# Attention under one named ScalarE table set, with the tanh of a row's gated input in three stretches a head later

## The chip, the core and the metric

One NeuronCore of a Trainium2 chip runs the whole network as one program. The time is the device time of one execution, in microseconds (us). Engines named below: PE (TensorE: matmuls, with PEld its weight loads), ACT (ScalarE: functions by table, copies, scalings), DVE (VectorE), POOL (GpSimd), SP (SyncE, which issues most DMAs). Each engine works through its own list of instructions in order; instructions on different engines wait for each other through semaphores.

## The reference, cut to what matters

Four rows (batch elements) of 512 tokens and 512 channels go through a Mamba-style layer, a mixture of experts, an attention layer and a feed-forward layer. Each layer takes its input through a gate, a bidirectional decayed sum over the tokens. Only the last two layers and the gate matter here:

```python
# the gate (r: the residual stream; k = v: a side input)
ek  = exp(minimum(k, 30)); ekv = ek * v
nf, df, nb, db = ...        # scans of ekv and ek over the tokens, both ways
euk = exp(minimum(u + k, 30))
num = nf + nb - ekv + euk * v
den = df + db - ek + euk
gate = sigmoid(r) * (num / maximum(den, 1e-8)) * (0.8 + 0.2 * tf)

# attention on h = gate(x): 16 heads in 4 groups, head size 128, causal
q = h @ w_q; k, v = split(h @ w_kv)
probs = softmax(where(causal, q @ k.T * scale, -inf))
x = x + (probs @ v) @ w_dense

# feed-forward on h = gate(x)
x = x + (silu((h @ gate_w.T) * gate_s) * ((h @ up_w.T) * up_s)) @ down_w.T * down_s
...
```

## The kernel before, in words

Everything is float32. Activations lie with the channels on the 128 partitions, in four chunks of 128, and the 512 tokens of a row along the free axis. A planner places the instructions of each engine: the program's order gives priorities, and an instruction goes to its engine's list when its inputs are expected; `after(engine)` and `issue_after` pin an instruction behind another.

**Table sets.** [...] The class `Tables` (lines 96 to 128) names sets explicitly: `act.use(set)` writes a load of the set behind every function called through `act(...)` since the last load, and every later `act(...)` is written behind that load. `LOG_EXP` has exp and ln, `EXP` has exp and tanh, `SILU` has silu and tanh. After `act.leave()` no set is named, and the compiler puts in whatever loads the list needs. In the kernel before, all of the mixture of experts, the attention and the feed-forward layer runs in that state. A call through `act(...)` is recorded at line 121 while no set is named and at line 125 while one is; a named load is recorded at line 112.

**Gates.** The generator `gate_pair` makes the x-independent factor of a gate for two of the four chunks of one row: two side inputs, four forward scans (L256) and four backward scans (L262) on DVE, the scaled copies `f` (L258) and the exponentials `eu` on ACT, then the division as three passes of ACT over 1024 elements (`rec`): a Relu (L313), a Ln and an Exp (both recorded at L121), and three products on DVE (L319, L323, L328). The result is stored to DRAM (L330). `nudge()` takes one step of this work; the attention calls it once for each 128-query block of each head. `have(gate)` takes steps until a named gate is complete. `gated(l, b, ...)` calls `have`, loads the finished factor (L395) and applies it: a tanh on ACT for each chunk (L121, from `xr` into `th`) and a product on DVE (L383).

**Attention** (lines 1498 to 1658). The 64 heads run in the order group, row, head of the group. In each turn of the loop:

- for the second head of a row in the first group, `combine(b + 1)` adds the expert results to the next row: a scaling on ACT (L1442), a sum on DVE (L1443), four PE transposes (`pcb`, L1448) and an addition to the residual (L1452), for each of four token blocks; right after it `gated(2, b + 1, ...)` makes the next row's input `h`;
- `begin(n + 1)` makes the next head's queries (`pq`, L1552; `qT`, L1560), and at a new row its keys and values (`pk`, L1530; `pv`, L1538);
- `scores`: for each of four query blocks one matmul (`psc`, L1569), the causal mask (L1572), the negated row maximum (`nmax`, L1574), then Exp on ACT with the row sum (L1579), a reciprocal (L1580) and a scaling (L1581);
- `context` of the head before: ten PE transposes (`ptp`, L1592), four copies (`pT`, L1595, on ACT or DVE as the planner likes), four matmuls (`pctx`, L1601) and a copy (`cx`, L1609);
- after the fourth head of a row, `dense` of that row: 16 matmuls (`pd`, L1616) and four additions (L1624).

`pk`, `pv`, `pq` and `psc` share four PSUM buffers (`mm`), taken in turn: a matmul into one of them waits until the Exp or copy that reads its previous content is done.

**Feed-forward** (lines 1661 to 1711). The weights `ffg`, `ffu`, `ffd` are loaded into the room that the attention leaves. For each row `gated(3, b, ...)`, then 11 pairs of matmuls (`pfg` L1678, `pfu` L1683), a Silu (L1687), a product (L1688) and the down projection (`pfo`, L1693).

## Time and profile before

| what | value |
|---|---|
| median of three runs (lowest to highest) | 2603.02 us (2601.29 to 2605.94) |
| the profiled execution's own time | 2605.88 us |
| its span, first to last instruction | 2604.2 us |
| attention, about 1173 to 2147 us of the span | PE busy 941.1 of 974 us, DVE 535.5, ACT 437.9 |
| feed-forward, 2147 to 2604 us | PE busy 452.7 of 457 us |
| loads of a table set in the attention | 20 around Ln (10 at L121, 10 at L1579), 1 before the first Silu, 1.28 us each |

All times below count from the start of the span. The span is 1.7 us shorter than the execution's own time, and the execution is 2.9 us above the median. A line of the timeline gives the start, the length, the engine, the line of the kernel, the operation, and in brackets the engine's idle time just before it and the instruction it waited for.

### The profile page before, as it was taken

The numbers are of one execution on the slowest core, as the hardware profiler recorded it, in microseconds if no ns is written. First come the engines' busy times: TensorE is split into PE (matmuls) and PEld (weight loads), VectorE is DVE, ScalarE is ACT, GpSimd is POOL, SyncE is SP. The second block draws the span as 40 slices with busy tenths as digits, with TensorE's granted clock in tenths as the row PEclk, the third lists the DMA queues.
The fourth block names the chain that finished last, engine by engine and source line by source line (L and its number), as shares of the span: only waits on it lengthen the run. The fifth ranks groups of instructions, "written<-read, shape, count | busy, mean of one in ns | idle before, by whom it ended". The sixth has DMA issues, their size and how long they took to land.

```text
span 2604.2 us, 24554 instructions
## 1 busy us (share of the span) xinstructions
PE 2450.3 (94%) x8204; PEld 1300.7 (50%) x8204; DVE 1412.3 (54%) x2788; ACT 1033.2 (40%) x2126; POOL 259.9 (10%) x299
## 2 busy tenths in 40 slices
PE   3889998999989999989999999999999999999999
PEld 1555555556544444435555555555555554444444
DVE  8798898996345565556666654556553441011010
ACT  4576757666123233224454444345443431000000
POOL 1031223322211121210000000000000000000000
PEclk9989999999899999999999999999999999999999
DMA  6222423324244697876221101111000012000000
GB/s 216 82 93 94 166 74 126 130 69 146 82 177 170 217 371 296 334 242 219 61 65 45 45 29 29 45 41 33 21 25 16 17 53 97 17 0 16 8 8 16
DMA packets 91391, 259.82 MB, mean 100 GB/s; under 512 B 9857, under 2 KB 19457, under 8 KB 80641
## 3 DMA queue, kind: packets, MB, share of 16 engines
q1 hardware_dynamic: 82080, 231.51, 25.5%
q0 software_dynamic: 6880, 22.55, 2.4%
q10 hardware_dynamic: 2304, 4.20, 0.4%
q8 instruction: 65, 1.06, 0.2%
q14 instruction: 62, 0.50, 0.1%
HBM read 284.82 MB, written 47.05 MB: 127 GB/s over the span
## 4 chain that ended last, share of the span: by engine, by line
PE 77%; DVE 14%; ACT 4%; DMA 3%; issue 2%; POOL 0%; SPq 0%; ACTq 0%; DVEq 0%; POOLq 0%
PE pd L1616 8%; PE pq L1552 7%; PE pfu L1683 6%; PE pfo L1693 6%; PE pfg L1678 6%; PE pctx L1601 5%; PE pn L774 5%; PE pg L763 5%; PE po L796 4%; PE pc L995 4%; PE psc L1569 3%; PE po L1223 3%; PE pv L1538 2%; PE ptp L1592 2%; PE pk L1530 2%; PE pz L1066 2%
## 5 line engine op out<-in xcount | busy, mean ns | idle before, releaser
L1552 PE MATMUL pq<-h,wq 128*128 128x512 f32 x512 | 249.4, 603 | 9.5 <-ACT pr L1579 9.4
L1616 PE MATMUL pd<-cx,wd 128*128 128x512 f32 x512 | 222.4, 592 | 0.0
L995 PE MATMUL pc<-h,wxb 128*128 128x512 f32 x320 | 150.0, 624 | 45.8 <-DVE h L1263 38.7
L1687 ACT ACTIVATE hd<-pfg,cols 128x512 f32<-128x512 f32 x44 | 30.3, 688 | 381.0 <-PE pfg L1678 381.0
L1688 DVE SCALAR_TENSOR_TENSOR hd<-pfu,cols,hd 128x512 f32<-128x512 f32 x44 | 33.0, 751 | 269.2 <-PE pfu L1683 269.1
L1572 DVE TENSOR_TENSOR psc<-psc,mask 128x128 f32<-128x128 f32 x256 | 71.7, 287 | 196.1 <-PE psc L1569 196.0
L1579 ACT ACTIVATE pr<-psc,nmax 128x128 f32<-128x128 f32 (+3 forms) x256 | 135.3, 529 | 98.1 <-DVE nmax L1574 97.3
L1601 PE MATMUL pctx<-pT,v 128*128 128x512 f32 (+3 forms) x512 | 155.9, 448 | 7.5 <-ACT pT L1595 4.0
L1683 PE MATMUL pfu<-h,ffu 128*128 128x512 f32 x352 | 158.7, 592 | 0.9 <-DMA ffu<-in_upT 0.9
L1678 PE MATMUL pfg<-h,ffg 128*128 128x512 f32 x352 | 158.6, 592 | 0.0
L796 PE MATMUL po<-w,yT 128*128 128x512 f32 x312 | 145.3, 607 | 12.7 <-ACT yT L789 12.7
L1569 PE MATMUL psc<-kT,qT 128*128 128x128 f32 (+3 forms) x512 | 151.8, 436 | 2.2 <-ACT qT L1560 1.2
L1616 PEld LDWEIGHTS pd<-cx,wd 128*128 128x128 f32 x512 | 96.1, 190 | 114.8 <-issue 110.5
L1693 PE MATMUL pfo<-hd,ffd 128*128 128x512 f32 x352 | 151.7, 592 | 0.0
L763 PE MATMUL pg<-w,hT 128*128 128x512 f32 x312 | 145.1, 605 | 6.7 <-DMA w<-in_w1x 6.7
L1601 PEld LDWEIGHTS pctx<-pT,v 128*128 128x128 f32 x512 | 94.6, 193 | 99.2 <-issue 37.4
L774 PE MATMUL pn<-w,hT 128*128 128x512 f32 x312 | 141.0, 593 | 1.7 <-DMA w<-in_w1x 1.7
L1624 DVE TENSOR_TENSOR xr<-xr,pd 128x512 f32<-128x512 f32 x64 | 44.0, 688 | 175.5 <-PE pd L1616 175.5
L1574 DVE TENSOR_REDUCE nmax<-psc 128x1 f32<-128x128 f32 (+3 forms) x256 | 123.4, 484 | 2.7
L1552 PEld LDWEIGHTS pq<-h,wq 128*128 128x128 f32 x512 | 87.8, 193 | 68.4 <-issue 57.4
L1592 PEld LDWEIGHTS ptp<-ident,pr 128*128 128x128 f32 x640 | 78.3, 143 | 86.9 <-issue 40.4
L995 PEld LDWEIGHTS pc<-h,wxb 128*128 128x128 f32 x320 | 61.8, 199 | 118.2 <-issue 73.0
(305 smaller groups left out, 4217.4 us busy)
## 6 DMA issues: line engine op xcount, KB each, us to landing
w<-in_w1x SPq DMA_DIRECT2D x80, 1024.0 KB
w<-in_w2x SPq DMA_DIRECT2D x40, 1024.0 KB
wb<-in_b1x SPq DMA_DIRECT2D x40, 512.0 KB
lm<-cs SPq DMA_DIRECT2D x32, 512.0 KB
kt<-in_fT SPq DMA_DIRECT2D x62, 256.0 KB
ek<-ek SPq DMA_DIRECT2D x62, 256.0 KB
ekv<-ekv SPq DMA_DIRECT2D x62, 256.0 KB
g<-num SPq DMA_DIRECT2D x30, 512.0 KB
```

Of the source, the lines that this page charges most:

```text
L763: nc.tensor.matmul(pg, lhsT=hT[:, k, :], rhs=self.w1[s][0][:, k, :], start=(k == 0), stop=(k == NC - 1))
L774: nc.tensor.matmul(pn, lhsT=hT[:, k, :], rhs=self.w1[s][1][:, k, :], start=(k == 0), stop=(k == NC - 1))
L796: nc.tensor.matmul(po, lhsT=yT[:, j, :], rhs=self.w2[s][:, j, :], start=(j == 0), stop=(j == NI - 1))
L995: nc.tensor.matmul(pc, lhsT=wxb[:, k, m * P : (m + 1) * P], rhs=h[:, k, :], start=(k == 0), stop=(k == NC - 1),)
L1552: nc.tensor.matmul(pq, lhsT=u.wq[:, k, i * KVC : (i + 1) * KVC], rhs=u.h[:, k, :], start=(k == 0), stop=(k == NC - 1),)
L1569: nc.tensor.matmul(psc[:, :n], lhsT=qT[:, qi * P : n], rhs=u.kT[:, :n], start=True, stop=True)
L1579: nc.scalar.activation(pr, psc[:, :n], AF.Exp, bias=nmax, accum_out=rsum)
L1601: nc.tensor.matmul(pctx[:, kj * P :], lhsT=u.v[:, kj, :], rhs=pT[:, kj, kj * P :], start=(kj == 0), stop=(kj == NT - 1),)
L1616: nc.tensor.matmul(po, lhsT=u.wd[:, i, m * P : (m + 1) * P], rhs=u.ctxT[i], start=(i == 0), stop=(i == HPG - 1),)
L1678: nc.tensor.matmul(pg, lhsT=wg[:, k, cs], rhs=h[:, k, :], start=(k == 0), stop=(k == NC - 1))
L1683: nc.tensor.matmul(pu, lhsT=wu[:, k, cs], rhs=h[:, k, :], start=(k == 0), stop=(k == NC - 1))
L1693: nc.tensor.matmul(po, lhsT=wdn[:, i, m * P : (m + 1) * P], rhs=hd[i], start=(i == 0), stop=(i == NFF - 1),)
```

## The change

The attention names its table sets. `LOG_EXP` is loaded ahead of the first head, and the Exp of the scores (L1579) and the Silu of the feed-forward layer (L1687) go through `act(...)`, so that they stand behind the named loads, too. `gated(2, b + 1, ...)` moves from the turn of a row's second head to that of its third, behind `begin(n + 1)`, between a load of `EXP` and a load of `LOG_EXP`; `combine(b + 1)` stays where it was. After the last head `SILU` is loaded.

```diff
-                nc.scalar.activation(pr, psc[:, :n], AF.Exp, bias=nmax, accum_out=rsum)
+                act(pr, psc[:, :n], AF.Exp, bias=nmax, accum_out=rsum)
...
+        with after(nc.scalar):
+            act.use(act.LOG_EXP)
         groups = {}
         ready, held = begin(0), None
         for n, (g, b, i) in enumerate(heads_):
             u, qT = ready
             if g == 0 and i == 1 and b + 1 < B:
                 combine(b + 1)
-                hs[b + 1] = gated(2, b + 1, x[b + 1], gp, tag="h", name=f"h2_{b + 1}")
             if n + 1 < len(heads_):
                 ready = begin(n + 1)
+            if g == 0 and i == 2 and b + 1 < B:
+                act.use(act.EXP)
+                hs[b + 1] = gated(2, b + 1, x[b + 1], gp, tag="h", name=f"h2_{b + 1}")
+                act.use(act.LOG_EXP)
             prs = scores(u, i, qT)
...
         for _ in making:
             pass
+        act.use(act.SILU)
...
-                nc.scalar.activation(hi, pg, AF.Silu, scale=col("gate_s", i))
+                act(hi, pg, AF.Silu, scale=col("gate_s", i))
```

## The prediction, made before the changed kernel ran

> **What bounds the kernel now.** I read the page's busy shares first, then its chain that ended last, then the chain inside the attention, then PE's and DVE's timelines. The first lines are the page's busy times, its chain by engine, one of its groups, and the attention as one window.

> ```profile
> PE 2450.3 (94%) x8204; PEld 1300.7 (50%) x8204; DVE 1412.3 (54%) x2788; ACT 1033.2 (40%) x2126; POOL 259.9 (10%) x299
> ...
> PE 77%; DVE 14%; ACT 4%; DMA 3%; issue 2%; POOL 0%; SPq 0%; ACTq 0%; DVEq 0%; POOLq 0%
> ...
> L1552 PE MATMUL pq<-h,wq 128*128 128x512 f32 x512 | 249.4, 603 | 9.5 <-ACT pr L1579 9.4
> ...
> 1173.00:2147.00 974.00, 941.13 (x3412) 522.82 (x3410) 535.52 (x1357) 437.92 (x1043) 2.85 (x4) 0.99 0.15 49
> ```

> PE sets the end. In the attention it stands still for only 974 - 941 = 33 us, so this is all that an ACT change can win there, plus what those halts cost in speed. Next, the chain in time around the second Ln:

> ```profile
> 1309.33 1.73 PE pq L1552 x4
> ...
> 1311.71 1.28 ACT L121
> ...
> 1313.00 1.15 ACT rec L121
> ...
> 1314.17 1.28 ACT L1579
> ...
> 1315.46 0.47 ACT pr L1579 x2
> ...
> 1315.97 1.12 PE pq L1552 x2
> ```

> Two table loads of 1.28 us stand around the Ln, an Exp of the scores stands behind them, and `pq` waits for the PSUM buffer which that Exp reads. PE's timeline has all halts of this kind (last bracket: idle time, releaser):

> ```profile
> 1315.97 1.12 PE L1552 MATMUL pq<-h,wq 128*128 128x512 f32 x2 [2.44 <-ACT pr L1579]
> 1543.49 1.98 PE L1552 MATMUL pq<-h,wq 128*128 128x512 f32 x4 [2.49 <-ACT pr L1579]
> 1616.57 0.98 PE L1592 MATMUL ptp<-ident,pr 128*128 128x128 f32 x7 [3.19 <-DVE pT L1595]
> 1618.59 3.68 PE L1601 MATMUL pctx<-pT,v 128*128 128x512 f32 x8
> 1703.00 4.12 PE L1601 MATMUL pctx<-pT,v 128*128 128x512 f32 x8 [2.48 <-DVE pT L1595]
> 1852.62 3.03 PE L1552 MATMUL pq<-h,wq 128*128 128x512 f32 x4 [2.49 <-ACT pr L1579]
> 1939.14 0.90 PE L1592 MATMUL ptp<-ident,pr 128*128 128x128 f32 x3 [2.65 <-DVE pT L1595]
> ```

> Six of the ten Ln halt PE by about two loads; at the other four (1227, 1376, 1460, 1770) PE halts 0.6 us at most. PE is also slower after the halts: `pctx` x8, otherwise 2.40, takes 4.12 and 3.68.

> [...] the Ln ends at 1314.15, the load starts at 1314.17. A pair costs 2.57. [...]

> **The change part by part.** I use the changed kernel's instruction order as compiled, with durations from the trace of before.

> *Removed: the 20 loads at Ln.* The order shows no load at any Ln. Each halt falls by the smaller of itself and 2.57: 2.44 + 2.49 + 2.57 + 2.48 + 2.49 + 2.57 = 15.0. The slow matmuls after them: at 1616, pq 1.41 for 1.02 and pctx 3.68 for 2.40, 1.7; at 1703, 4.12 for 2.40, 1.7; at 1852, pq 3.03 for 1.88, ptp 0.85 for 0.49, pq 1.40 for 1.02, 1.9; at 1939, ptp 0.90 for 0.49, pq 1.91 for 1.02, ptp 0.91 for 0.60, 1.6; the other two 0.2. Together 7.1, and 22.1 with the halts. The three `rec` passes (1.15 + 1.15 + 1.05) stay, in or around one head of about 9 us of PE work, so some halt may remain: bounds 15 and 22, and I take 20.

> *Added: eight loads.* The first `LOG_EXP` comes between the two halves of row 0's tanh, and the compiler puts a load back behind it: 2.57 on ACT from 1182.4. The last two tanh end at 1186.1 instead of 1183.4, their products by 1187.0, and `pk` wants its third chunk at 1187.9 (and has a `pq` matmul in front of it now). Cost 0, if that cover were gone up to 2. The `SILU` load replaces the compiler's, and is early.

> *Feed-forward tanh moved.* Those of rows 0 to 2 ran during dense; they must now follow the `SILU` load, that is the last Exp (ends 2124.5). Load to 2125.8; of the 12 tanh, two stand before the `cx` of the last head but one (due 2127.0), two before the last `pT` (2128.4), four before the last `cx` (2131.5). Each waits for a DVE product of 0.69, which also delays a `pT` on DVE by 0.5. PE gets its last `pctx` about 0.5 late; the rest lies under 13.9 us of dense. SP's DMAs for `h` and the weights do not wait for these tanh. Cost 0.5 (0 to 2).

> *Three tanh stretches: a barrier.* Every Exp of the third head now waits for its row's four tanh and two loads; queued behind them are `pT` and `cx` copies. PE then lacks the buffer for `pk`, since the four are held by that head's `psc`.

> Row 1: load 1217.8 to 1219.1, four tanh among the `pT` copies, the last to 1222.6, load to 1223.9, first Exp done 1224.4; `pk` was due at 1225.1. The last `pT` for `pctx` ends at 1222.1, as before. Cost 0 (to 1).

> Row 2: Exp of the fourth block to 1281.2, load to 1282.5, two tanh to 1283.6, a scaling and a `cx` to 1284.8, two tanh (held by DVE products) to 1286.0, load to 1287.3, Exp to 1287.8. PE reaches `pk` at about 1284.3 and idles 3.6. Before, it lost 0.74 + 1.23 there and 0.6 of speed, and in the new order it has `pctx` done already: `pv` starts at about 1294.5 against 1294.95. A halt this long brings the slow matmuls, 1.7 as above. Cost 1.5 (-1 to 3).

> Row 3 is the dear one. Here `have` is called a head later, and the order moves the gate's last products behind the dense additions. Before, they were done ahead of dense (DVE's timeline):

> ```profile
> 1316.90 1.23 DVE L319 SCALAR_TENSOR_TENSOR den<-den,rec 128x1024 f32<-128x1024 f32 x1
> ...
> 1321.50 1.28 DVE L323 SCALAR_TENSOR_TENSOR num<-num,tf_out,rec 128x1024 f32<-128x1024 f32 x1
> ...
> 1323.29 1.22 DVE L328 SCALAR_TENSOR_TENSOR num<-den,num 128x1024 f32<-128x1024 f32 x1
> ```

> Let D be the end of that dense (1338.2 before). Ahead of the second head's fourth row maximum DVE now has, from D + 0.9: three `xr` additions 1.96, four masks 1.05, four maxima 1.90, one scan 1.22, these three products 3.73, the `rr` sum 0.75, three scalings 1.04 and three reciprocals 0.45, in all 12.1, less 1.6 since neighbours overlap by 0.08: D + 11.4. Then ACT: Exp to 12.2, load to 13.4; PE: third `psc` of the next head to 12.8, `pctx` to 15.0; ACT: `cx` to 15.7, two tanh to 16.8, three `pT` to 18.2; PE: second `pctx` to 20.4; ACT: `cx` to 21.1, two tanh to 22.2, load to 23.4, `f` to 24.1, Exp to 24.5; only now `pk`. With `pk` 3.4 and `pv` 3.6 PE is at D + 31.5. Before it took 1360.6 - 1338.2 = 22.4, with three `psc` (1.3) done ahead of dense. So 31.5 - 22.4 - 1.3 = 7.8 more, and 1.7 for slow matmuls after the 4 us halt: 9.5 (3 to 12). The `rr` load that ACT awaited 10.4 us at 1341.6 is hidden by dense either way.

> Sum: -20 + 0 + 0.5 + 0 + 1.5 + 9.5 = -8.5. The profiled execution becomes 2605.88 - 8.5 = 2597.4; as that one is 2.9 above the median, I predict 2603.0 - 8.5 = 2594.5.

> **The rivals.** *A: row 3's barrier is covered.* If the gate's products do not delay the row maxima, it costs about 2, and the sum is -16: 2587. For it: DVE is idle within dense. Against it: the products stand behind dense's additions in the list. *B: the halts at Ln half refill.* DVE's row maxima and the `rec` passes remain; three of the six halts already name a DVE copy as releaser. The gain is then 10 and the sum +1.5: 2604.5. Against it: the halts have almost exactly two loads' length. *C, slower: the barrier costs in all rows what it does in row 3.* One head's Exp all wait for tanh, tanh for `combine`, and `pk` for an Exp. At 9.5 for each row it is 28.5 + 0.5 - 20 = +9: 2612. It decides from 6.5 a row upwards. For it: DVE was the tight engine there at rows 2 and 3; against it: row 1's walk ends with room.

> **How the numbers follow.** Forecast 0.48 (own range -14 to -3), A 0.15, B 0.22, C 0.15. A measurement of this kernel tells about 0.2%, 5.2 us, from no change. Faster by more: A and three quarters of the forecast, 0.51. Within: the rest of the forecast and 0.17 of B, 0.29. Slower: C and 0.05 of B, 0.20. The range 2586 to 2609 leaves out the fast half of A and most of C.

> **What would show it.** In the profile after: no load near any `rec`; no PE halt of 2.4 or more after 1400; loads in the attention down from 21 to 9; a PE halt of 3 to 4 before `pk` of row 2, and of about 4, with 4 to 5 more shortly before it, at row 3; DVE's L319 to L328 behind dense there. Halts at Ln from row maxima or `pT`, or a halt before `pk` of row 1, would make it wrong.

## The result, and the profile after

| | before | after |
|---|---|---|
| median of 12 runs each (lowest to highest), us | 2606.17 (2601.21 to 2610.90) | 2596.11 (2588.45 to 2599.37) |
| ratio, with its 95% interval | | 0.9957 (0.9945 to 0.9968) |
| span of the profiled execution, us | 2604.2 | 2592.2 |

The ratio is 11.2 us less (8.3 to 14.3): faster, by about twice what a measurement of this kernel tells from no change. Forecast were 8.5 us less. In the lines of the changed kernel the Exp of the scores stands at L125, the feed-forward matmuls at L1685 to L1700. First the page: busy times, the chain by engine, and the group of the queries' matmuls with its idle time at the end.

```profile
PE 2446.9 (94%) x8204; PEld 1299.2 (50%) x8204; DVE 1412.7 (54%) x2792; ACT 1012.7 (39%) x2110; POOL 260.4 (10%) x299
...
PE 75%; DVE 15%; ACT 4%; DMA 3%; issue 2%; POOL 0%; SPq 0%; ACTq 0%; DVEq 0%; POOLq 0%
...
L1552 PE MATMUL pq<-h,wq 128*128 128x512 f32 x512 | 247.3, 597 | 2.1 <-ACT pr L125 2.0
```

ACT lost 20.5 us of work, PE hardly any; but the idle time in front of `pq` fell from 9.5 to 2.1 us. PE's timeline of the changed kernel shows where the other halts went:

```profile
1209.13 5.40 PE L1552 MATMUL pq<-h,wq 128*128 128x512 f32 x8 [2.03 <-ACT pr L125]
...
1285.87 2.07 PE L1530 MATMUL pk<-h,wkv 128*128 128x512 f32 x2 [3.23 <-ACT pr L125]
...
1357.66 6.58 PE L1530 MATMUL pk<-h,wkv 128*128 128x512 f32 x8 [4.10 <-ACT pr L125]
...
1733.43 0.66 PE L1592 MATMUL ptp<-ident,pr 128*128 128x128 f32 x4 [0.96 <-ACT pT L1595]
```

The first line stood in the kernel before as well (2.03 us at 1211.04, no Ln near it). From 1400 to the end of the attention no halt is longer than the 0.96 of the last line; before there were five of 2.5 to 3.2 there. Two long halts are new, both in front of `pk`, waiting for an Exp: the stretches of rows 2 and 3.

The first `pk` of the attention comes at 1185.96 before and at 1184.07 after, and in the profiled executions below anywhere from 1181.2 to 1191.9, though nothing upstream of it was edited. So spans are compared from there on. The attention is cut at the first matmul of row 0's `dense` and of row 3's in the first group, and at that of the last `dense`. (Each piece holds the same matmuls in all nine kernels.) Piece one holds row 1's stretch, piece two those of rows 2 and 3, and piece three has none. Nine of the ten Ln lie in pieces two and three; of the six that halted PE, one (at 1316) did in piece two and five in piece three.

| kernel (us) | first `pk` to `dense` row 0 | to `dense` row 3 | to last `dense` | sum |
|---|---|---|---|---|
| before | 68.9 | 183.8 | 692.7 | 945.4 |
| after | 68.8 | 193.2 | 672.7 | 934.8 |
| moved only, tables by the compiler | 68.4 | 187.7 | 691.4 | 947.4 |
| no stretch, sigmoid by Exp and Ln | 73.1 | 186.2 | 672.4 | 931.7 |
| gate completed early | 68.8 | 185.1 | 671.6 | 925.5 |
| stretch behind `scores` | 73.3 | 185.9 | 672.7 | 931.8 |
| stretch at the second head | 75.4 | 188.7 | 671.7 | 935.8 |
| sigmoid by Exp and Ln at the second head | 70.8 | 193.1 | 671.7 | 935.6 |
| mixed | 68.9 | 184.0 | 671.7 | 924.6 |

The third column falls into two levels. Where the compiler chooses the tables it is 691 to 693; where they are named it is about 672, whatever else is done. That is the gain. The second column is where most of it was given back, and what the experiments are about.

PE loses time there in two ways: it stands still, and it runs slowly afterwards. The trace records the clock granted to PE, here either 1.00 or 0.50. These are neighbouring stretches of 3.41 us around row 2's halt, first in the changed kernel, then in the run with the gate completed early (start and end, length, PE's busy time with its matmuls, granted clock, share of DMA, GB/s):

```profile
1281.57:1284.99 3.42, 1.07 (x5) 1.00 0.30 77
1284.99:1288.40 3.41, 2.53 (x6) 0.50 0.00 0
1288.40:1291.82 3.42, 3.42 (x9) 0.50 0.00 0
1291.82:1295.23 3.41, 3.41 (x12) 1.00 0.29 82
...
1286.38:1289.79 3.41, 1.57 (x8) 1.00 0.31 85
1289.79:1293.20 3.41, 2.02 (x7) 1.00 0.01 4
```

Both halts last 3.23 us. The first leaves one stretch mostly idle, and PE then runs 6.83 us at half clock; the second is split over two stretches, and the clock stays. What the traces show of this stands in the last section. So a part of a difference between two traces can be the clock alone. The next table has it apart: the time from the end of a `dense` to the end of the `pv` that follows it, that is, over the stretch and the halt of a row. In brackets are the time that PE idled in it and the time at half clock.

| kernel (us) | row 2 | row 3 |
|---|---|---|
| before | 29.9 (2.2, 3.4) | 22.4 (0.7, none) |
| after | 32.2 (3.6, 6.8) | 33.2 (6.2, 6.8) |
| moved only, tables by the compiler | 27.3 (1.1, none) | 30.0 (3.0, 3.4) |
| no stretch, sigmoid by Exp and Ln | 29.7 (2.8, none) | 28.7 (4.3, none) |
| gate completed early | 29.3 (3.4, none) | 28.1 (2.7, 3.4) |
| sigmoid by Exp and Ln at the second head | 33.6 (5.2, 6.8) | 31.8 (4.9, 6.8) |
| mixed | 29.7 (2.8, none) | 27.4 (2.0, none) |

The work in a column is the same, but for row 3: the kernel before has 1.3 us less there (scores that it makes ahead of `dense`), the runs "moved only" and "mixed" about 1 us more (a pair of query matmuls). So row 3 is measured against 22.4 + 1.3 = 23.7.

### The profile page after: what moved, and what is told of

The parts are those of the page before. It is cut to its first block, busy times and chain, and to the rows that moved or that the text cites. A ratio compares the mean times of both kernels' runs of the same rounds, so it can differ in the third digit from the quotient of the medians.

```text
span 2592.2 us, 24553 instructions
## 1 busy us (share of the span) xinstructions
PE 2446.9 (94%) x8204; PEld 1299.2 (50%) x8204; DVE 1412.7 (54%) x2792; ACT 1012.7 (39%) x2110; POOL 260.4 (10%) x299
## 4 chain that ended last, share of the span: by engine, by line
PE 75%; DVE 15%; ACT 4%; DMA 3%; issue 2%; POOL 0%; SPq 0%; ACTq 0%; DVEq 0%; POOLq 0%
PE pd L1616 8%; PE pq L1552 7%; PE pfu L1690 6%; PE pfo L1700 6%; PE pfg L1685 6%; PE pctx L1601 5%; PE pn L774 5%; PE pg L763 5%; PE po L796 4%; PE psc L1569 3%; PE pc L995 3%; PE pv L1538 2%; PE po L1223 2%; PE ptp L1592 2%; PE pz L1066 2%; PE pk L1530 2%
## 5 line engine op out<-in xcount | busy, mean ns | idle before, releaser
L1552 PE MATMUL pq<-h,wq 128*128 128x512 f32 x512 | 247.3, 597 | 2.1 <-ACT pr L125 2.0
L125 ACT ACTIVATE hd<-pfg,cols 128x512 f32<-128x512 f32 x44 | 30.2, 687 | 382.9 <-PE pfg L1685 382.9
L125 ACT ACTIVATE pr<-psc,nmax 128x128 f32<-128x128 f32 (+3 forms) x256 | 135.2, 529 | 84.5 <-DVE nmax L1574 83.8
L1685 PE MATMUL pfg<-h,ffg 128*128 128x512 f32 x352 | 158.8, 593 | 0.0
L1601 PE MATMUL pctx<-pT,v 128*128 128x512 f32 (+3 forms) x512 | 152.6, 441 | 4.8 <-ACT pT L1595 3.8
L1700 PE MATMUL pfo<-hd,ffd 128*128 128x512 f32 x352 | 151.7, 592 | 0.0
L1624 DVE TENSOR_TENSOR xr<-xr,pd 128x512 f32<-128x512 f32 x64 | 44.0, 687 | 178.8 <-PE pd L1616 178.8
L1601 PEld LDWEIGHTS pctx<-pT,v 128*128 128x128 f32 x512 | 93.4, 190 | 93.5 <-issue 36.3
L1560 ACT ACTIVATE qT<-pq 128x512 f32<-128x512 f32 x64 | 38.2, 597 | 253.8 <-PE pq L1552 253.8
L1592 PEld LDWEIGHTS ptp<-ident,pr 128*128 128x128 f32 x640 | 77.5, 142 | 85.7 <-issue 38.6
```

Of the source, the lines that this page charges most:

```text
L125: nc.scalar.activation(*args, **kw)
L1552: nc.tensor.matmul(pq, lhsT=u.wq[:, k, i * KVC : (i + 1) * KVC], rhs=u.h[:, k, :], start=(k == 0), stop=(k == NC - 1),)
L1601: nc.tensor.matmul(pctx[:, kj * P :], lhsT=u.v[:, kj, :], rhs=pT[:, kj, kj * P :], start=(kj == 0), stop=(kj == NT - 1),)
L1685: nc.tensor.matmul(pg, lhsT=wg[:, k, cs], rhs=h[:, k, :], start=(k == 0), stop=(k == NC - 1))
L1700: nc.tensor.matmul(po, lhsT=wdn[:, i, m * P : (m + 1) * P], rhs=hd[i], start=(i == 0), stop=(i == NFF - 1),)
```

## Experiments

Two lots were run, each next to the kernel before (medians 2605.26 of 27 runs and 2606.29 of 19). Ratios are to that.

**The move alone.** The kernel before, with `gated` at the third head and no set named: the loads at every Ln stay.

```diff
                 combine(b + 1)
-                hs[b + 1] = gated(2, b + 1, x[b + 1], gp, tag="h", name=f"h2_{b + 1}")
             if n + 1 < len(heads_):
                 ready = begin(n + 1)
+            if g == 0 and i == 2 and b + 1 < B:
+                hs[b + 1] = gated(2, b + 1, x[b + 1], gp, tag="h", name=f"h2_{b + 1}")
```

> The kernel before with the later place of the gated input alone: no named set, no stretch, the 20 compiler loads at Ln stay. Theory (the gain is the loads at Ln, about 20 us, and the barrier of the tanh stretches takes about 10 back): five or six PE halts of 2.4 to 3.2 us at the Ln remain, pk of row 3 waits less than 2 us, and the time is that of before within 4 us (ratio 0.999 to 1.0015). Rival 1 (row 3 loses through the later place, since the gate's last products pile up on VectorE, not through the stretch): slower by 6 to 10 us, ratio 1.002 to 1.004. Rival 2 (the gain comes from the later place): faster by 5 us or more, ratio below 0.998.

Measured: 2609.35 us, ratio 1.0011 (1.0002 to 1.0020). Its PE still halts at the Ln; two of these halts in its timeline:

```profile
1642.91 3.63 PE L1552 MATMUL pq<-h,wq 128*128 128x512 f32 x4 [2.49 <-ACT pr L1579]
1717.43 1.31 PE L1592 MATMUL ptp<-ident,pr 128*128 128x128 f32 x7 [3.19 <-DVE pT L1595]
```

The third column stays at 691.4. So the gain comes from the loads, not from the new place, which by itself costs about 3 us (0.5 to 5.2). Its row 3 loses about 5 (30.0, less 1 for the two query matmuls, against 23.7), and its row 2 wins 2.6, 1.1 of it idle time and the rest the clock. So the first rival had row 3 right: the later place costs there without any named set; only its total is too large.

**No stretch.** The changed kernel without its loads of `EXP`: the gate's sigmoid of rows 1 to 3 is built from functions of `LOG_EXP` (sigmoid(r) = exp(-ln(1 + exp(-r)))), three ACT instructions for each tanh. One load of `LOG_EXP` stands ahead of the first of them.

```diff
-                act.use(act.EXP)
-                hs[b + 1] = gated(2, b + 1, x[b + 1], gp, tag="h", name=f"h2_{b + 1}")
-                act.use(act.LOG_EXP)
+                hs[b + 1] = gated(
+                    2, b + 1, x[b + 1], gp, exps=True, tag="h", name=f"h2_{b + 1}"
+                )
...
+            act(th, xs[:, cc, :], AF.Exp, scale=-1.0)
+            act(th, th, AF.Ln, bias=1.0)
+            act(th, th, AF.Exp, scale=-1.0)
```

> The changed kernel without the three stretches: the gate of rows 1 to 3 takes its sigmoid by Exp, Ln and Exp in the set that is loaded anyway (three passes of ScalarE for each tanh, 24 more in all, about 15 us), so that no Exp of the scores stands behind a load; six loads fewer, one more to come back to the set once. Theory: the halts at Ln stay away and row 3's loss of 9.5 us falls below 3: ratio to before 0.992 to 0.994 (the changed kernel: 0.9957). Rival 1: row 3 still loses 6 or more, since VectorE's pile is unchanged: ratio 0.995 to 0.997. If the added passes are what ScalarE cannot take: new halts of PE at rows 1 to 3 behind qT or pT, ratio 0.996 or more.

Measured: 2591.12 us, ratio 0.9946 (0.9933 to 0.9960), just above what the theory allows. The pieces say more: 7.0 us are won in rows 2 and 3 against the changed kernel, and 4.3 are lost in row 1. Row 3 still loses 5.0 (28.7 against 23.7), between the theory's 3 and the first rival's 6. In row 1 PE halts in front of `pk`, where the changed kernel didn't:

```profile
1218.13 2.08 PE L1541 MATMUL pk<-h,wkv 128*128 128x512 f32 x2 [2.77 <-ACT pr L125]
```

There the third head's Exp stand behind eight more ACT instructions and one load, where the changed kernel has two loads, and 6.8 us at half clock begin with this halt. In rows 2 and 3 the loads were the worse of the two: about 2.7 of the 7.0 us are idle time of PE, and most of the rest is that it no longer falls to half clock.

**The gate completed early.** The changed kernel, with `have` called right behind `combine`, a head ahead of the stretch.

```diff
                 combine(b + 1)
+                have((2, b + 1))
```

> The changed kernel with the gate's own work asked for at its old place (with combine, one head ahead of the stretch), so that its last products stand ahead of dense again. Theory by my walk (the fourth row maximum 3.7 us earlier, the chain of loads, tanh, cx and pT unchanged): row 3 loses 4 to 6 instead of 9.5, ratio to before 0.993 to 0.995. Rival 1 (the pile is all of it): row 3 loses 1 or less, ratio 0.992. Rival (the pile is hidden, the stretch is all of it): as the changed kernel, 0.9957.

Measured: 2589.63 us, ratio 0.9933 (0.9920 to 0.9946). DVE's timeline of the changed kernel around the last `dense` addition of row 1 (L1624), ahead of row 3's stretch, shows what this moves; the last line is the row maximum that the second head's last Exp waits for:

```profile
1334.65 0.69 DVE L1624 TENSOR_TENSOR xr<-xr,pd 128x512 f32<-128x512 f32 x1 [2.75 <-PE pd L1616]
...
1338.18 1.20 DVE L319 SCALAR_TENSOR_TENSOR den<-den,rec 128x1024 f32<-128x1024 f32 x1
...
1340.54 1.28 DVE L323 SCALAR_TENSOR_TENSOR num<-num,tf_out,rec 128x1024 f32<-128x1024 f32 x1
...
1343.32 1.22 DVE L328 SCALAR_TENSOR_TENSOR num<-den,num 128x1024 f32<-128x1024 f32 x1
...
1345.04 0.69 DVE L1574 TENSOR_REDUCE nmax<-psc 128x1 f32<-128x512 f32 x1
```

With the gate early, the same view has the products ahead of the first of the dense additions:

```profile
1317.86 1.20 DVE L319 SCALAR_TENSOR_TENSOR den<-den,rec 128x1024 f32<-128x1024 f32 x1
...
1324.89 1.23 DVE L328 SCALAR_TENSOR_TENSOR num<-den,num 128x1024 f32<-128x1024 f32 x1
...
1327.23 0.69 DVE L1624 TENSOR_TENSOR xr<-xr,pd 128x512 f32<-128x512 f32 x1 [0.46 <-PE pd L1616]
```

and its PE waits less at row 3, while the halt at row 2 keeps its length:

```profile
1291.18 1.13 PE L1530 MATMUL pk<-h,wkv 128*128 128x512 f32 x2 [3.23 <-ACT pr L125]
...
1354.05 1.52 PE L1530 MATMUL pk<-h,wkv 128*128 128x512 f32 x2 [1.75 <-ACT pr L125]
```

The second piece falls from 193.2 to 185.1. Of these 8.1 us, 5.1 are row 3's (33.2 to 28.1; 3.5 of it idle time, the rest the clock): that is what the three gate products cost there, left behind `dense`, in front of the row maxima. Row 3 still loses 4.4, as the theory had it (4 to 6). Row 2's 2.9 are not the products' doing as far as is seen: its halt has the same length, and only the clock differs, 6.8 us at half rate against none. How often row 2 meets the half clock isn't known from one trace of each kernel. By the medians the edit is worth about 6 us.

Nor are the products alone the cause. The run without a stretch has them as late as the changed kernel, leaves the loads out instead, and comes nearly as low in row 3 (28.7). Either takes about 5 us off; with both ("mixed", below) it is 27.4, so the two don't add up. In the forecast's walk they stand ahead of the same Exp.

**The stretch behind `scores`.** The changed kernel, with the third head's scores issued ahead of the stretch, so that they need not stand behind it.

```diff
+            prs = scores(u, i, qT)
             if g == 0 and i == 2 and b + 1 < B:
...
-            prs = scores(u, i, qT)
```

> The changed kernel with each stretch behind the scores of the same head instead of ahead of them: that head's Exp no longer wait for tanh, and pk of the next row waits for the tanh and their products, not for a PSUM buffer. Theory: at rows 2 and 3 the halt before pk falls from 3.2 and 4.1 us to below 2.5, the slow matmuls behind it shrink: ratio to before 0.993 to 0.995. Rival 1: only VectorE's pile counts, so row 3 still loses 8 or more: 0.9955 or higher.

Measured: 2595.68 us, ratio 0.9961 (0.9946 to 0.9976): no better than the change. Rows 2 and 3 gain 7.4 us in its profile, row 1 loses 4.4. The ratio lies in the rival's range, but the loss isn't where the rival had it. In row 1 the first Ln now comes ahead of the first stretch. The compiler had put a load back for the second half of row 0's tanh (at 1182.14, 0.01 us behind the first named one), and this Ln has its pair of loads again (1223.98 and 1226.45). With the stretch's two (1228.54 and 1233.13) four loads stand within 11 us. By medians 3 to 4 us of the profile's gain are missing. Its profiled execution is 4.8 us below the kernel's median, that of the changed kernel 2.2 below its own, which makes up 2.6; the rest is open.

**The stretch at the second head.** The changed kernel with everything of `gated`, and its loads, right behind `combine`.

```diff
                 combine(b + 1)
-            if n + 1 < len(heads_):
-                ready = begin(n + 1)
-            if g == 0 and i == 2 and b + 1 < B:
                 act.use(act.EXP)
                 hs[b + 1] = gated(2, b + 1, x[b + 1], gp, tag="h", name=f"h2_{b + 1}")
                 act.use(act.LOG_EXP)
+            if n + 1 < len(heads_):
+                ready = begin(n + 1)
```

> The changed kernel with its stretch (EXP load, gated, LOG_EXP load) right behind combine, at a row's second head, not a head later. The gate's products then come a head earlier, as before the change, but the four tanh wait for combine's last addition, and every Exp of the second head stands behind them. Theory (the head's delay is there for combine, and it pays): PE halts longer in front of a matmul that wants that head's Exp, over 3 us in at least two of the three rows; from the first pk to the first dense of row 3 the attention is not shorter than in the changed kernel; ratio to the kernel before 0.995 to 1.000. Rival (only the time of the gate's products matters, the place of the stretch doesn't): as with the gate completed early, the ratio is 0.992 to 0.9945, and row 3 has no halt over 2 us.

Measured: 2597.44 us, ratio 0.9966 (0.9954 to 0.9978). PE halts in row 1 in the middle of `combine`, and in row 2 in front of `pctx`; row 3, at 1.12, is the exception:

```profile
1217.53 1.09 PE L1448 MATMUL pcb<-ident,rr 128*128 128x128 f32 x4 [6.11 <-DVE rr L1443]
...
1289.81 4.61 PE L1601 MATMUL pctx<-pT,v 128*128 128x512 f32 x8 [3.04 <-DVE pT L1595]
```

The gate is as early here as in the run with `have` early, so these two differ by the head alone: 935.8 against 925.5 us. Giving the tanh out a head later is worth about 10 us in these traces, about 8 by the medians; the change spoils part of it, since `have` went along.

**The sigmoid at the second head.** No stretches as above, and `gated` at its old place.

```diff
                 combine(b + 1)
+                hs[b + 1] = gated(
+                    2, b + 1, x[b + 1], gp, exps=True, tag="h", name=f"h2_{b + 1}"
+                )
...
-            if g == 0 and i == 2 and b + 1 < B:
-                act.use(act.EXP)
-                hs[b + 1] = gated(2, b + 1, x[b + 1], gp, tag="h", name=f"h2_{b + 1}")
-                act.use(act.LOG_EXP)
```

> No stretches: the gate's sigmoid of rows 1 to 3 by Exp, Ln and Exp in LOG_EXP, and gated at its old place, right behind combine, so that the gate's products stand ahead of dense again. ACT has 12 instructions of about 0.55 us for a row in place of four, and no load there. Theory (row 3 lost by the two loads' barrier and by the products behind dense, both gone here): first dense of row 0 to that of row 3 is 182 to 186 us (183.8 before, 193.2 after the change), and the ratio is 0.991 to 0.9935. Rival (the cost is ACT's work between combine and pk, of whatever kind): eight more ACT instructions, about 4.4 us in each row, cost PE what the loads did: over 188 us there, ratio at or above 0.995.

Measured: 2595.13 us, ratio 0.9957 (0.9942 to 0.9972). My theory is refuted and the rival's numbers hold (193.1 us in the second piece). No load stands in rows 2 and 3, the gate is early, and yet as much is lost as in the changed kernel, with as much idle time (5.2 and 4.9 us) and the half clock in both rows. What ACT does at the second head, loads or functions, holds up the Exp behind it.

**Mixed.** The gate early, the stretch for row 1 alone, and for rows 2 and 3 the sigmoid without loads at the third head.

```diff
                 combine(b + 1)
+                have((2, b + 1))
...
-                act.use(act.EXP)
-                hs[b + 1] = gated(2, b + 1, x[b + 1], gp, tag="h", name=f"h2_{b + 1}")
-                act.use(act.LOG_EXP)
+                if b == 0:
+                    act.use(act.EXP)
+                hs[b + 1] = gated(
+                    2, b + 1, x[b + 1], gp, exps=b > 0, tag="h", name=f"h2_{b + 1}"
+                )
+                if b == 0:
+                    act.use(act.LOG_EXP)
```

> A candidate for the best: the gate completed early (right behind combine), the tanh stretch for row 1 alone, where the changed kernel lost nothing, and for rows 2 and 3 the sigmoid by Exp, Ln and Exp a head later, without loads. Theory (in rows 2 and 3 what is left of the loss is the two loads, 2.57 us of ACT in front of an Exp that pk waits for): no halt before pk over 2 us in row 2 or 3, where the gate completed early alone showed 3.23 and 1.75; first dense of row 0 to that of row 3 181 to 184 us against 185.1; ratio 0.991 to 0.993. Rival (the eight extra ACT instructions of a row, about 4.4 us, take the place of the 2.57 us of loads): the same halts or longer ones, 185 us or more, and a ratio of 0.993 to 0.996.

Measured: 2585.80 us, ratio 0.9923 (0.9907 to 0.9938), below both kernels. The halts before `pk` in rows 2 and 3 are down to 1 us, and wait for the product on DVE, no longer for an Exp:

```profile
1292.83 1.13 PE L1541 MATMUL pk<-h,wkv 128*128 128x512 f32 x2 [1.01 <-DVE h L394]
...
1355.73 1.13 PE L1541 MATMUL pk<-h,wkv 128*128 128x512 f32 x2 [1.02 <-DVE h L394]
```

The second piece is 184.0, at the edge of what was expected, 1.1 us below the early gate alone; PE keeps its full clock through all of it. The intervals of these two ratios overlap: which is faster isn't settled; that both beat the changed kernel by their medians is seen, and for this one the intervals don't meet.

## Why the prediction was right, point by point

- **The loads at Ln (forecast -20).** Right, a little short. Third piece -19.9, and the halt of 2.44 at 1316 in the second piece is gone too: about -22, the upper bound, which was the halts plus the slow matmuls after them. Both are seen in the third piece: PE's idle time falls from 19.2 to 6.8 us, and four stretches of 3.41 us at half clock are gone. I estimate their cost at half of their length, 6.8 together; the prediction counts 6.9 in the slow matmuls after these four halts. The reserve for halts that stay (rival B) wasn't needed: the `rec` passes alone stop PE nowhere for more than 0.96 us after 1400. Of the steps, no load stands near any `rec`, and the attention has nine loads.
- **Eight added loads, row 1 (0 and 0).** Right: the first piece is 68.9 before and 68.8 after, with two loads in it and two just ahead of it. The cover is thin: eight more functions (no stretch), or two more loads (stretch behind `scores`), cost 4 us there.
- **Feed-forward tanh (0.5).** From the last `dense` to the end of the span it is 472.8 before and 473.4 after: right.
- **Row 2 (1.5).** Somewhat short: from `dense` to the end of `pv` 29.9 before and 32.2 after, 2.3 us. PE waits 3.23 before `pk`, where 3.6 was forecast, but runs 6.8 us at half clock where the forecast's 1.7 us is worth one stretch of 3.41. (For the kernel before, the forecast names 0.6 us of lost speed there; by the same estimate the stretch at half clock cost it 1.7. As the forecast compares instants, its sum doesn't depend on this.) With row 3's 9.5 and the vanished halt the second piece comes out: 2.3 + 9.5 - 2.4 = 9.4, as measured.
- **Row 3 (9.5).** The sum is right, two terms are off against each other. The forecast's instants, from where PE leaves `dense` (1334.45 in this trace), against ACT's timeline:

```profile
1345.77 0.69 ACT L125 ACTIVATE pr<-psc,nmax 128x512 f32<-128x512 f32 x1 [1.01 <-DVE nmax L1574]
...
1346.56 1.28 ACT L112 ACT_TABLE_LOAD   x1
...
1354.08 1.15 ACT L125 ACTIVATE th<-xr 128x512 f32<-128x512 f32 x2
1355.24 1.28 ACT L112 ACT_TABLE_LOAD   x1
...
1357.16 0.35 ACT L125 ACTIVATE pr<-psc,nmax 128x128 f32<-128x128 f32 x1
```

The last maximum ends at D + 11.3 (forecast 11.4), the first load at D + 13.4 (13.4), `pk` starts at D + 23.2 (24.5). The walk ran 1.3 long: of the "4 to 5 shortly before", PE idled only about 2, besides the 4.10 in front of `pk`. But the slow matmuls cost 3.0 and not 1.7: `pk` x8 takes 6.58 against 3.60 in row 1 of the same trace, since the clock stayed at half for two stretches of 3.41 us and not for one. `pv` is done at D + 33.2, which is the forecast's 31.5 and 1.7: the two errors cancel, and that is luck. Rival A (this barrier covered) and C (as dear in every row) are out; and with the early gate, which takes the products out of the way of the row maxima, row 3 still loses 4.4, where A had about 2.
- **The base.** The forecast stood on the median of three runs, 2603.0; twelve gave 2606.2. The 8.5 from there would be 2597.7. So the close hit of 2594.5 is helped by a base that was 3 us low and a gain that was 2 to 3 us too small.

What was not forecast is how much of the cost could be removed by one line. The prediction named both causes (`have` called a head later, and the barrier of the loads) and charged them with 9.5 together; taking out either one removes about 5 of it.

## What to carry to other kernels

When an in-order engine works with switched tables, count the halts that a switch causes in the bound engine, not the engine's own busy time: here 20 loads of 1.28 us gave 22 us since PE stood behind six of the ten pairs and ran slowly after four of them. When a step is given out later, look at everything that the call brings along: the tanh gained from a head's delay, the products that came with them lost by it, and splitting the call kept most of the one without the other. Before a few us between two traces are put down to an edit, compare the granted clock in both. Price a barrier by what is queued around it at that moment: here the same four tanh and two loads cost nothing in row 1, and with the late products 9.5 us in row 3.
